# A four-layer graph network on one NeuronCore: about half of layer 3's dense products placed inside layer 2, with seven running-maximum blocks and 13 dense node tiles

## The chip, the cores and the metric

The kernel runs on one NeuronCore of a Trainium2 chip. Its engines are TensorE (PE: matrix products; PEld: the loading of the stationary operand), VectorE (DVE), ScalarE (ACT), GpSimd (POOL) and SyncE (SP). SP and ACT issue plain DMAs, POOL issues the indirect ones (gathers by a list of row numbers); all of them are carried by the same 16 DMA engines. The metric is device time in microseconds for one execution.

## What is computed

6250 nodes, 100 000 edges sorted by destination, features of 256, hidden width 512. A node's degree falls with its number (the destinations are drawn as the square of a uniform number), so the first nodes collect most of the edges of a tile.

```python
h = relu(layernorm(x))
h = sage_mean(h)   # h @ W1_self + mean over in-edges of h[src] @ W1_neigh + b1
h = sage_pool(h)   # hp = relu(h @ W2_pool + b2_pool); max over in-edges of hp[src];
                   # h @ W2_self + max @ W2_neigh + b2
h = sage_gcn(h)    # ((sum over in-edges of h[src]) + h) / (deg + 1) @ W3_neigh + b3
h = sage_mean(h)   # with W4_self, W4_neigh, b4
out = x + h @ W_fc + b_fc
```

Nothing nonlinear stands behind the maximum of layer 2, so the kernel multiplies the weights of layers 2 to 4 and the last one together beforehand: layer 3 works on a table of 512 columns that is the output of layer 2 times those products, layer 4 on one of 256.

## The kernel before

**Tiles.** The nodes make 49 tiles of 128 rows (NT), the edges 782 tiles of 128 (T). A table row that is summed on PE is kept as three bf16 parts (`parts`, L266: two ACT casts, two DVE subtractions), so each product over it is three matmuls: `tab_h` for layer 1, `tab_r` for layer 3 (3 x 512 columns, 3072 bytes a row), `tab_s` for layer 4 (3 x 256 columns).

**Two ways of summing edges (layers 1, 3 and 4).** The first node tiles, with many edges each, are *dense*: `build` (L280) makes, for a node tile d, the count matrix between its nodes and each source tile and writes it to the DRAM table `tab_a[d]`, 49 blocks of 128 x 128 bf16; `dense` (L401) then multiplies each block with the rows of source tile s, three matmuls for each s, and adds up over the 49 source tiles in one PSUM bank. The other node tiles are summed by `sums` (L337): for each edge tile POOL gathers the 128 source rows into a ring, DVE makes a one-hot matrix of the destinations, PE multiplies (three matmuls), four edge tiles share one PSUM bank (a group), and DVE adds the group into the node tiles that it may belong to. `HUB = (8, 9, 18)` gives the number of dense node tiles in layers 1, 3 and 4. The gathers of layer 3 thus begin at the edge group of node tile 9 (454 edge tiles), those of layer 4 at that of node tile 18 (314 edge tiles). The dense work is spread between the gathers by `Hub.advance` (L326); `wait` says after how many gathers it begins (40 in layer 3, 24 in layer 4).

**Layer 2 (L835 to L1080)** takes a maximum. For all 782 edge tiles POOL gathers 128 rows of 2 KB of `tab_p` (L1051) into a buffer `X` of two tiles (8 such buffers), DVE carries the running maximum (L1056), SP writes each pair to the DRAM table `runb` (512 KB, L1069). The edge tiles are cut into five blocks, `BLOCKS = (288, 208, 144, 88, 54)`. When a block is through, `block_end` (L1018) runs for it, in small steps beside the gathers of the next block, one step for each edge tile: `carry` (L937) passes the maximum across the block's partitions, `totals` (L979) gathers the result rows `tot` of each node tile that ends in the block and loads `th` from `tab_t`, and `done2` (L992) transposes them, makes the own part (`usA`, `usB`, L1005 and L1007) and the neighbour part (`un`, L1010) in fp32, splits the result into three parts and writes `tab_r[d]` (L1016). What has not run when the next block ends is issued then in one piece. The last block closes seven node tiles (42 to 48) behind the last gather. In layer 2 the builds of dense tiles 8 to 17 are placed too (L1061), and at its start the weight products (`products2`, L905).

**Layer 3 (L1122 on)** starts when `tab_r` is written: it loads all 49 tiles of it into SBUF (`resident`, L1113: seven DMAs of 2.7 MB on SP's queue), streams the dense blocks (`stream`, L1085: seven source tiles a DMA, on ACT's queue), and runs `sums` with the dense work of nine node tiles beside it. `done3` (L1134) adds the node's own row (three matmuls with an identity: L419 inside `dense` for dense tiles, L1142 for the others), writes `tab_s` and, with x added, `xq`. **Layer 4** does the same on `tab_s` with 18 dense tiles and writes `out`.

**Order.** The instructions are written down in the order of the Python code, and the framework's scheduler then fixes an order for each engine and each issuing queue, with times of its own for each instruction; every engine takes its instructions in that fixed order and waits for what is not ready.

Of the kernel before, what the change touches and what calls it, by code (L numbers as in the profile page):

```python
# [9 lines left out]
F32 = mybir.dt.float32  # L10
# [14 lines left out]
G = 4  # L25
BLOCKS = (288, 208, 144, 88, 54)
Z_SIGMA = 5.0
WIN = 8
HUB = (8, 9, 18)
# [38 lines left out]
def fast_path(  # L68
# [155 lines left out]
    def product(wp, pst, psm, w, rhs, put):  # L224
        k_n = w.shape[1] // P
        for m in range(w.shape[0] // P):
            wl = wp.tile([P, k_n * P], F32, name="wl", bufs=2)
            nc.scalar.dma_start(wl, w[m * P : (m + 1) * P, :])
            wT = wp.tile([P, k_n, P], F32, name="wT", bufs=2)
            pt = bank(pst, "pt", "pt_w", (k_n, P))  # L230
            for k in range(k_n):
                nc.tensor.transpose(pt[:, k, :], wl[:, k * P : (k + 1) * P], ident)
            nc.scalar.copy(wT, pt)
            pm = bank(psm, "pm", "pm_w", (rhs.shape[2],))
            for k in range(k_n):
                nc.tensor.matmul(pm, wT[:, k, :], rhs[:, k, :],
                                 start=(k == 0), stop=(k == k_n - 1))
            nc.scalar.copy(put[:, m, :], pm)
            yield
# [76 lines left out]
    class Hub:  # L316


        def __init__(self, work):
            self.work = [w if isinstance(w, tuple) else (None, w) for w in work]  # L320
            self.hot_at = [i for i, w in enumerate(self.work) if w[0]]
            self.done = 0
            self.hot = 0
            self.passed = 0

# [75 lines left out]
    def dense(d, block, rows, F, psd, todo, done, extra=0, self_term=False):  # L401

        hold = {}

        def run(s):
            if s == 0:
                hold[0] = bank(psd, "pd", "pd", (F + extra,))
            a = block(s)
            z = rows(s)
            for part in (2, 0, 1):  # L410
                c = extra if part == 2 else 0
                nc.tensor.matmul(hold[0][:, : F + c], a, z[:, part * F : (part + 1) * F + c],  # L412
                                 start=(s == 0 and part == 2),
                                 stop=(s == NT - 1 and part == 1 and not self_term))
            if s == NT - 1:
                if self_term:
                    z = rows(d)
                    for part in range(3):
                        nc.tensor.matmul(hold[0], ident_b, z[:, part * F : (part + 1) * F],  # L419
                                         start=False, stop=(part == 2))  # L420
                todo.append(done(d, hold[0]))

        return [lambda s=s: run(s) for s in range(NT)]
# [293 lines left out]
    with ExitStack() as on:  # L717
# [10 lines left out]
        def done1(d, acc):  # L728
# [23 lines left out]
            for k in range(KI):  # L752
# [11 lines left out]
        denses = [dense(d, lambda s, A=As[d % 2]: A[:, s, :], h0_row, FI, psd, todo, done1,  # L764
                        extra=1) for d in range(H1)]
# [68 lines left out]

    with tc.tile_pool(name="fl2c", bufs=1) as ck, ExitStack() as late:  # L835
        pst = late.enter_context(tc.tile_pool(name="pst2", bufs=2, space=PSUM))
        psm = late.enter_context(tc.tile_pool(name="psm2", bufs=3, space=PSUM))
# [96 lines left out]
        wpool = late.enter_context(tc.tile_pool(name="fw2", bufs=1))  # L934
        wk = late.enter_context(tc.tile_pool(name="fl2", bufs=2))

# [42 lines left out]
        def totals(d):  # L979
            tots = []  # L980
            for b in range(b_of[d][0], b_of[d][1] + 1):
                t = wk.tile([P, FH], F32, name="tot", bufs=6)
                nc.gpsimd.indirect_dma_start(
                    out=t, out_offset=None, in_=runs[b],
                    in_offset=bass.IndirectOffsetOnAxis(ap=rows_of[b][:, d : d + 1], axis=0),
                )
                tots.append(t)
            th = wk.tile([P, 2 * KI, P], F32, name="th2", bufs=3)
            nc.scalar.dma_start(th, tab_t[d].rearrange("p (k n) -> p k n", n=P))
            return tots, th  # L990

        def done2(d, got):  # L992
            tots, th = got
            hm = tots[0]
            for t in tots[1:]:
                nc.vector.tensor_tensor(hm, hm, t, op=ALU.max)
            pt = bank(pst, "pt", "pt_hTf", (KH, P))
            for j in range(KH):
                nc.tensor.transpose(pt[:, j, :], hm[:, j * P : (j + 1) * P], ident)
            hT = wk.tile([P, KH, P], F32, name="hTf")  # L1000
            nc.scalar.copy(hT, pt)  # L1001
            yield
            pm = bank(psm, "pm", "pm_prf")
            for k in range(KI):
                nc.tensor.matmul(pm, th[:, k, :], usA[:, k, :], start=(k == 0), stop=False)  # L1005
            for k in range(KI):
                nc.tensor.matmul(pm, th[:, KI + k, :], usB[:, k, :], start=False, stop=False)  # L1007
            yield
            for c in range(KH):
                nc.tensor.matmul(pm, hT[:, c, :], un[:, c, :], start=False, stop=(c == KH - 1))  # L1010
            pr = wk.tile([P, FH], F32, name="prf")
            nc.vector.tensor_add(pr, pm, prow)
            yield
            r3 = wk.tile([P, 3 * FH], BF16, name="r3")
            parts(pr, FH, r3)
            nc.sync.dma_start(tab_r[d * P : (d + 1) * P, :], r3)  # L1016

# [17 lines left out]
        steps = products2(wpool)  # L1035
        A = wk.tile([P, NT, P], BF16, name="A", bufs=1)
        work = []
        for d in range(H1, H4):
            work += build(d, A, (skR, mkR, RB1), wk, psb)
        hub = Hub(work)  # L1040
# [3 lines left out]
        for b, tb in enumerate(BLOCKS):  # L1044
            t0 = offs[b] // P
            for s0 in range(0, tb, G2):
                n = min(G2, tb - s0)
                X = wk.tile([P, G2, FH], F32, name="X2", bufs=8)
                for k in range(n):
# [13 lines left out]
                    hub.advance(math.ceil(len(work) * max(0, t - 60) / (T - 100)))  # L1063
# [15 lines left out]
        for _ in end:  # L1079
            pass  # L1080


    CH = 7

    def stream(pool, h, check):  # L1085

        got = {}

        def load(i):
            if i >= h * (NT // CH):  # L1090
                return
            d, c = divmod(i, NT // CH)
            t = pool.tile([P, CH, P], BF16, name="ac", bufs=5)
            nc.scalar.dma_start(t, tab_a[d, :, c * CH : (c + 1) * CH, :])
            got[d, c] = t
# [9 lines left out]
        def block(d, s):  # L1105
            c, r = divmod(s, CH)
            if r == 0:
                load(d * (NT // CH) + c + 4)
            return got[d, c][:, r, :]
# [3 lines left out]
    def resident(pool, table, F):  # L1113
        zt = pool.tile([P, NT, 3 * F], BF16, name="zt", bufs=1)
        for i0 in range(0, NT, CH):
            nc.sync.dma_start(  # L1116
                zt[:, i0 : i0 + CH, :],
                table[i0 * P : (i0 + CH) * P, :].rearrange("(c p) f -> p c f", p=P),
            )
        return zt  # L1120

    with ExitStack() as on:  # L1122
        ek = on.enter_context(tc.tile_pool(name="fe3", bufs=1))
        jb = g_of[H3][0] * G
        srcT = ek.tile([P, T - jb], I32, name="srcT3")
        nc.scalar.dma_start(srcT, stash_e[0, :, jb:T].bitcast(I32))
        keyT = ek.tile([P, T - jb], F32, name="keyT3")
        nc.scalar.dma_start(keyT, stash_e[1, :, jb:T])
        psd = on.enter_context(tc.tile_pool(name="psd3", bufs=2, space=PSUM))
        psg = on.enter_context(tc.tile_pool(name="psg3", bufs=3, space=PSUM))  # L1130
        psm = on.enter_context(tc.tile_pool(name="psm3", bufs=2, space=PSUM))

        with tc.tile_pool(name="fl3", bufs=2) as wk:
            def done3(d, acc):  # L1134
                q = wk.tile([P, FH], F32, name="q", bufs=2)
                if d < H3:
                    nc.vector.scalar_tensor_tensor(q, acc, rgcn[:, d : d + 1], qrow,
                                                   op0=ALU.mult, op1=ALU.add)
                else:
                    own = bank(psm, "pm", "pm_own")  # L1140
                    for part in range(3):
                        nc.tensor.matmul(own, ident_b, Z3[:, d, part * FH : (part + 1) * FH],  # L1142
                                         start=(part == 0), stop=(part == 2))
# [12 lines left out]
                nc.sync.dma_start(xq[d * P : d * P + n, :], xr[:n, :])  # L1156

            Z3 = resident(wk, tab_r, FH)
            block = stream(wk, H3, False)
            todo = []  # L1160
            work = []
            for d in range(H3):
                work += dense(d, lambda s, d=d: block(d, s), lambda s: Z3[:, s, :], FH, psd,
                              todo, done3, self_term=True)
            sums(wk, psg, tab_r, FH, srcT, keyT, jb, H3, done3, 7, Hub(work), wait=40, todo=todo)

        with tc.tile_pool(name="fl4", bufs=2) as wk:
# [9 lines left out]
            Z4 = resident(wk, tab_s, FO)  # L1177
            block = stream(wk, H4, True)
            todo = []
            work = []  # L1180
            for d in range(H4):
                work += dense(d, lambda s, d=d: block(d, s), lambda s: Z4[:, s, :], FO, psd,
                              todo, done4)
            sums(wk, psg, tab_s, FO, srcT, keyT, jb, H4, done4, 14, Hub(work), wait=24, todo=todo)
# [643 lines left out]
```

## Time and profile before

Three runs took 3241.90, 3242.98 and 3246.33 us (median 3242.98). The profiled execution took 3257.08 us, of which the span from the first to the last instruction is 3255.3 us.

| engine | busy us | share of the span |
|---|---|---|
| PE | 2334.0 | 72% |
| PEld | 1334.9 | 41% |
| DVE | 1858.8 | 57% |
| ACT | 887.4 | 27% |
| POOL | 2155.6 | 66% |

The stages, by the first and last gather of each: layer 1's gathers start at 145.2 and end at 788.7 us, layer 2's run from 827.5 to 2017.4, layer 3's from 2127.0 to 2795.0, layer 4's from 2815.0 to 3218.1.

In the profile an instruction is named by line, engine, operation and the tiles it writes and reads (out<-in). A PE matmul's duration is modelled and overlaps with its neighbours; the spacing of two of them is shorter. "PEclk" is the share of TensorE's clock that was granted. The DMA share is the mean busy share of the 16 DMA engines, and can exceed 1 a little, since packets overlap.

### The profile page before, as it was taken

How to read it: one execution, taken by the hardware profiler on the slowest of the kernel's cores; microseconds unless marked ns; L12 is line 12 of the kernel's file. 1: busy time of each engine (PE TensorE's matmuls, PEld its weight loads, DVE VectorE, ACT ScalarE, POOL GpSimd, SP SyncE). 2: the span in 40 equal slices, each digit the busy share in tenths (PEclk: the TensorE clock that was granted, in tenths of full speed). 3: DMA queues.
4: the chain of work that ended last, by engine and by line, in shares of the span. 5: the costliest groups of instructions: out<-in, count | busy, mean ns of one | idle time of the engine just before them, and what ended most of it. 6: DMA issues, size and time to landing. Idle time of an engine off the chain costs nothing. (4 is left out here: it accounts for less than half of the span.)

```text
span 3255.3 us, 39649 instructions
## 1 busy us (share of the span) xinstructions
PE 2334.0 (72%) x11991; PEld 1334.9 (41%) x12048; DVE 1858.8 (57%) x4764; ACT 887.4 (27%) x2367; POOL 2155.6 (66%) x2368
## 2 busy tenths in 40 slices
PE   2368999999483115410673677967999999799997
PEld 1134666666331002100231333422444444388886
DVE  4855666554656656655656665223566666566443
ACT  1557767663233223431234221200000000000000
POOL 5374777764567777777776776145766766577773
PEclk9678999999796556655786788989999999899999
DMA  5454677775999999999999999399999999888885
GB/s 178 162 156 139 212 217 222 241 221 177 324 386 405 394 386 375 409 399 382 380 397 407 393 406 388 119 355 355 346 336 340 345 338 352 289 288 271 259 263 167
DMA packets 394117, 991.17 MB, mean 304 GB/s; under 512 B 54799, under 2 KB 133729, under 8 KB 391558
## 3 DMA queue, kind: packets, MB, share of 16 engines
q0 software_dynamic: 155200, 557.74, 49.6%
q1 hardware_dynamic: 180788, 350.69, 28.6%
q10 hardware_dynamic: 57906, 80.12, 7.4%
q8 instruction: 98, 1.61, 0.2%
q14 instruction: 125, 1.02, 0.1%
HBM read 674.14 MB, written 315.00 MB: 304 GB/s over the span
## 5 line engine op out<-in xcount | busy, mean ns | idle before, releaser
L1051 POOL DMA_INDIRECT X<-tab_p,srcIf x782 | 836.0, 1069 | 314.5 <-issue 149.7
L374 PE MATMUL pg<-ring,hot 128*128 128x256 bf16 (+2 forms) x3697 | 780.5, 318 | 115.6 <-DMA ring<-tab_h,srcT 36.2
L412 PE MATMUL pd<-zt,ac 128*128 128x256 bf16 (+1 forms) x3944 | 696.5, 309 | 3.6 <-DMA zt<-tab_s 1.2
L302 PE MATMUL pb<-hm,hs 128*128 128x392 bf16 x781 | 280.4, 402 | 492.6 <-ACT A L306 292.7
L356 POOL DMA_INDIRECT ring<-tab_r,srcT x454 | 440.1, 969 | 277.4 <-PE pg L374 184.0
L356 POOL DMA_INDIRECT ring<-tab_h,srcT x474 | 452.1, 954 | 197.1 <-PE pg L374 80.5
L374 PEld LDWEIGHTS <-hot 128*128 128x128 bf16 x3726 | 367.7, 99 | 404.3 <-issue 175.7
L352 DVE TENSOR_SCALAR hot<-iota_bf,keyT 128x128 bf16<-128x128 bf16 x1242 | 310.2, 268 | 326.2 <-PE pg L374 314.1
L412 PEld LDWEIGHTS <-ac 128*128 128x128 bf16 x3969 | 389.4, 98 | 189.8 <-issue 3.4
L393 DVE SCALAR_TENSOR_TENSOR acc<-pg,M,acc 128x257 f32<-128x257 f32 (+2 forms) x567 | 306.9, 577 | 254.2 <-PE pg L374 253.5
L1056 DVE SCALAR_TENSOR_TENSOR X<-X,samef,X 128x512 f32<-128x512 f32 x386 | 289.4, 750 | 214.3 <-DMA X<-tab_p,srcIf 99.2
L1056 DVE SCALAR_TENSOR_TENSOR X<-X,samef 128x512 f32<-128x512 f32 x391 | 293.2, 750 | 184.8 <-DMA X<-tab_p,srcIf 181.0
L356 POOL DMA_INDIRECT ring<-tab_s,srcT x314 | 298.2, 950 | 125.0 <-PE pg L374 61.1
L294 ACT ACTIVATE hs<-ht,onef 128x128 bf16<-128x128 bf16 x781 | 289.8, 397 | 135.1 <-PE pb L302 134.4
L302 PEld LDWEIGHTS <-hs 128*128 128x128 bf16 x781 | 78.6, 105 | 597.7 <-issue 338.1
L306 ACT CAST A<-pb 128x392 bf16<-128x392 f32 x288 | 136.9, 480 | 438.1 <-DMA tab_a<-A 239.6
L1010 PE MATMUL pm_prf<-unf,hTf 128*128 128x512 f32 x392 | 198.6, 655 | 27.2 <-ACT hTf L1001 27.2
L296 DVE TENSOR_SCALAR hm<-iota_w,mk 128x392 bf16<-128x392 f16 x461 | 154.7, 341 | 62.5 <-PE pb L302 60.0
L269 ACT CAST q<-q 128x256 bf16<-128x256 f32 x49 | 19.8, 405 | 622.6 <-DVE q L1146 504.0
L412 PE MATMUL pd<-Z,A 128*128 128x256 bf16 (+1 forms) x1176 | 188.1, 274 | 0.1
L292 ACT ACTIVATE ht<-iota_bf,sk 128x128 bf16<-128x128 bf16 x461 | 171.8, 396 | 17.1 <-DVE bad L679 10.5
L1010 PEld LDWEIGHTS pm_prf<-unf,hTf 128*128 128x128 f32 x392 | 82.2, 214 | 148.2 <-issue 100.9
(272 smaller groups left out, 2321.0 us busy)
## 6 DMA issues: line engine op xcount, KB each, us to landing
runb<-X SPq DMA_DIRECT2D x391, 512.0 KB
ac<-tab_a ACTq DMA_DIRECT2D x189, 224.0 KB
tab_a<-A SPq DMA_DIRECT2D x18, 1568.0 KB
tab_r<-r SPq DMA_DIRECT2D x49, 384.0 KB
zt<-tab_r SPq DMA_DIRECT2D x7, 2688.0 KB
tab_t<-th SPq DMA_DIRECT2D x49, 256.0 KB
tab_p<-hpf SPq DMA_DIRECT2D x49, 256.0 KB
th<-tab_t ACTq DMA_DIRECT2D x49, 256.0 KB
```

The costliest lines, as they stand in the source:

```text
L292: nc.scalar.activation(t, iota_b, AF.Abs, bias=sk[:, r : r + 1])
L294: nc.scalar.activation(hots[0], t, AF.Relu, bias=one, scale=-1.0)
L296: nc.vector.tensor_scalar(hots[1], iota_w, mk[:, r : r + 1], None, op0=ALU.is_equal)
L302: nc.tensor.matmul(hold[0], hots[0], hots[1], start=(k == 0), stop=(k == k_of[w] - 1))
L352: nc.vector.tensor_scalar(hot[j], iota_b, keyT[:, j - jb : j - jb + 1], None, op0=ALU.is_equal)
L356: nc.gpsimd.indirect_dma_start(out=ring[:, j % deep, : 3 * F], out_offset=None, in_=table, in_offset=bass.IndirectOffsetOnAxis(ap=srcT[:, ...
L374: nc.tensor.matmul(pg[:, : F + c], hot[j], X[:, part * F : (part + 1) * F + c], start=(k == 0 and part == 2), stop=(k == n - 1 and part == 1),
L393: nc.vector.scalar_tensor_tensor(acc[d], pg, m, acc[d], op0=ALU.mult, op1=ALU.add)
L412: nc.tensor.matmul(hold[0][:, : F + c], a, z[:, part * F : (part + 1) * F + c], start=(s == 0 and part == 2), stop=(s == NT - 1 and part = ...
L1010: nc.tensor.matmul(pm, hT[:, c, :], un[:, c, :], start=False, stop=(c == KH - 1))
L1051: nc.gpsimd.indirect_dma_start(out=X[:, k, :], out_offset=None, in_=tab_p, in_offset=bass.IndirectOffsetOnAxis(ap=srcI[:, t : t + 1], axis=0),
L1056: nc.vector.scalar_tensor_tensor(X[:, k, :], prev, same[:, t : t + 1], X[:, k, :], op0=ALU.mult, op1=ALU.max,)
```

## The change

The first 24 of the 49 source tiles (EARLY) of layer 3's dense products are multiplied inside layer 2: as soon as four node tiles' rows `r3` are made (still in SBUF), `early_products` appends, for each of the 13 dense node tiles, one load of four blocks of `tab_a` (128 KB, on SP's queue) and four times three matmuls into a PSUM bank, and `add3` adds the bank to an SBUF accumulator `acc3[d]` (DVE; the first addition to each is an ACT copy). The own row of a dense tile goes into `acc3` the same way, so L419 goes. Layer 3 has 13 dense tiles (HUB 8, 13, 18), so its gathers begin at node tile 13: 386 edge tiles. It keeps 25 source tiles resident (five DMAs of 2.0 MB) and loads the own rows of node tiles 13 to 23 one by one (`zown`). There are seven blocks; the last closes node tiles 46 to 48, the one before it 41 to 45. The own parts of `done2` of the last eight node tiles are made in the middle of layer 2 (`own_terms`). Dense builds for tiles 8 to 12 are moved to the first 208 edge tiles. Three of the seven pieces of `tab_s` are loaded for layer 4 during layer 3, and layer 4's dense work begins with them, after 4 gathers instead of 24. Buffers change: X 8 to 6 pairs, `tot` 6 to 4, `th2` 3 to 2, PSUM banks `pm` 3 to 2 with two new ones for the early products, `wT` 2 to 1, `r3` 2 to 9.

```diff
-BLOCKS = (288, 208, 144, 88, 54)
+BLOCKS = (232, 184, 136, 100, 72, 38, 20)
-HUB = (8, 9, 18)
+HUB = (8, 13, 18)
+EARLY = 24
+OWN = 8
+OWN_AT = 64
...
+    def add3(d, v):
+
+        if d in begun:
+            nc.vector.tensor_add(acc3[d], acc3[d], v)
+        else:
+            begun.add(d)
+            nc.scalar.copy(acc3[d], v)
...
+        def own_terms():
+            for d in own:
+                th = load_th(d)
+                for _ in range(4):
+                    yield
+                pm = bank(psm, "pm", "pm_own2")
+                self_product(pm, th, True)
+                nc.vector.tensor_add(own[d], pm, prow)
+                yield
...
-            r3 = wk.tile([P, 3 * FH], BF16, name="r3")
+            if d < H3:
+                add3(d, pr)
+            r3 = early_pool[0].tile([P, 3 * FH], BF16, name="r3", bufs=2 * BATCH + 1)
             parts(pr, FH, r3)
             nc.sync.dma_start(tab_r[d * P : (d + 1) * P, :], r3)
+            if d < EARLY:
+                ready.append((d, r3))
+                if len(ready) == BATCH or d == EARLY - 1:
+                    early_products()
...
+                def load(d=d, got=got):
+                    got[0] = early_pool[0].tile([P, BATCH, P], BF16, name="ae", bufs=LOOK + 3)
+                    nc.sync.dma_start(got[0][:, : len(ss), :],
+                                      tab_a[d, :, ss[0] : ss[-1] + 1, :])
+
+                work = dense(ss, lambda s, got=got: got[0][:, s - ss[0], :],
+                             lambda s: batch[s], FH, psd, lambda v, d=d: add3(d, v))
+                early.add([(load, work[0])] + work[1:])
...
-                X = wk.tile([P, G2, FH], F32, name="X2", bufs=8)
+                X = wk.tile([P, G2, FH], F32, name="X2", bufs=6)
...
-                    hub.advance(math.ceil(len(work) * max(0, t - 60) / (T - 100)))
+                    if t > OWN_AT and t % 2:
+                        next(owns, None)
+                    if t <= begin:
+                        hub.advance(math.ceil(len(first) * max(0, t - 16) / (begin - 16)))
+                    else:
+                        hub.advance(len(first)
+                                    + math.ceil(len(rest) * (t - begin) / (T - 60 - begin)))
+                    early.advance(early.done
+                                  + max(1, math.ceil(early.left() / max(8, T - 30 - t))))
...
                 if d < H3:
-                    nc.vector.scalar_tensor_tensor(q, acc, rgcn[:, d : d + 1], qrow,
+                    nc.vector.tensor_add(q, acc, acc3[d])
+                    nc.vector.scalar_tensor_tensor(q, q, rgcn[:, d : d + 1], qrow,
                                                    op0=ALU.mult, op1=ALU.add)
                 else:
+                    if d in Z3:
+                        z = Z3[d]
+                    else:
+                        z = wk.tile([P, 3 * FH], BF16, name="zown", bufs=2)
+                        nc.sync.dma_start(z, tab_r[d * P : (d + 1) * P, :])
+                        yield 1
+                        yield 1
+                        yield 1
...
+                for s0, s1 in z4_early:
+                    if d == s1 - 1:
+                        Z4.update(resident(zk, tab_s, FO, s0, s1))
+            late_s = range(EARLY, NT)
...
-            sums(wk, psg, tab_r, FH, srcT, keyT, jb, H3, done3, 7, Hub(work), wait=40, todo=todo)
+            sums(wk, psg, tab_r, FH, srcE, keyE, jb, H3, done3, 7, Hub(work), wait=14, todo=todo)
...
-            sums(wk, psg, tab_s, FO, srcT, keyT, jb, H4, done4, 14, Hub(work), wait=24, todo=todo)
+            sums(wk, psg, tab_s, FO, srcE, keyE, jb, H4, done4, 14, Hub(work), wait=4, todo=todo)
```

## The prediction, made before the changed kernel was run

> **What bounds the kernel now.** I read the page's slices first, then the busy times by stage (stretches cut at the first and last gather of each stage; columns: stretch, length, then busy us and instruction count of each engine, granted PE clock, DMA share, GB/s), then the costs of single instructions, last the chain of waits where stages meet.
>
> ```profile
> PE   2368999999483115410673677967999999799997
> POOL 5374777764567777777776776145766766577773
> GB/s 178 162 156 139 212 217 222 241 221 177 324 386 405 394 386 375 409 399 382 380 397 407 393 406 388 119 355 355 346 336 340 345 338 352 289 288 271 259 263 167
> ```
> ```profile
> 1240.00:1975.00 735.00, 369.97 (x894) 155.10 (x893) 462.58 (x821) 221.58 (x602) 555.92 (x520) 0.70 1.03 394
> 2020.00:2127.00 107.00, 96.95 (x262) 45.00 (x261) 36.61 (x63) 23.93 (x42) 13.46 (x14) 0.97 0.44 155
> 2140.00:2250.00 110.00, 79.76 (x309) 30.54 (x314) 30.83 (x81) 0.81 (x2) 59.28 (x62) 0.94 1.02 400
> 2260.00:2795.00 535.00, 527.90 (x2404) 239.53 (x2452) 337.07 (x810) 35.30 (x88) 370.47 (x382) 1.00 0.96 341
> 2858.00:3236.00 378.00, 376.09 (x3444) 336.94 (x3444) 190.92 (x592) 0.00 (x0) 265.51 (x280) 1.00 0.83 258
> ```
>
> Layer 2 (first two lines above: 827 to 2127 us). While it gathers, PE is half idle, but two others are full: the DMA engines (share 1.03, 394 GB/s), and POOL, whose 520 indirect DMAs took 556 us and are 0.30 us apart at the least, so 712 of 735 us. Its gathers average 1.07 us against 0.95 in layer 4: in the trace's records those that overlap no two-input DVE instruction of L1056 take 0.96, those overlapped for over half 1.12 to 1.17. After the last gather (2017.4) 110 us pass until the first of layer 3 (2127.0), and that time is PE's:
>
> ```profile
> 2087.72 3.43 PE pm_prf L1010 x8
> 2091.15 0.44 PE pt_hTf L999 x4
> 2091.59 1.72 PE pm_prf L1005 x4
> 2093.31 1.72 PE pm_prf L1007 x4
> ```
> One node tile costs 0.44 + 3.44 (own part) + 3.43 (neighbour part) = 7.3 us, and some twelve stand in a row there.
>
> Layer 3 begins at the DMA limit (400 GB/s, while 19.3 MB of `zt` load) with one long wait, then from 2260 on PE is full at clock 1.00. Layer 4 loses its first 43 us to loads of `zt`, then PE is full again:
>
> ```profile
> 2223.42 30.24 DMA xq<-xrf
> ...
> 2796.85 0.65 PE pd L412 x3
> ...
> 2842.09 29.40 DMA zt<-tab_s
> ```
> The middle line gives the spacing of a 512-column matmul: 0.65 / 3 = 0.2157 us. In layer 4, (2646 + 942) matmuls of 256 columns at 0.1093 us (9 + 3 of them in 1.31 us on the chain) make 392 us.
>
> **Layer 3, part by part.** Gathers fall from 454 to 386, dense matmuls from 9 x 49 x 3 = 1323 (+27 own) to 13 x 25 x 3 = 975, own matmuls of the others from 120 to 108. PE: 975 + 3 x 386 + 108 = 2241 against 2832, at 0.2157 us 483 against 611. Two other bounds come close. POOL: 386 x (0.97 + 0.30) = 490 us (440.1/454 is this gather's mean). DMA: 386 gathers of 393 KB (151.8 MB), dense blocks 13 x 25 x 32.8 KB (10.7), `zt` 9.8, eleven `zown` 4.3, `tab_s`, `xrf`, `xq` 22.4, early `tab_s` pieces 4.1: 203 MB, against 235 now.
>
> Here a rule speaks against the change. The Trainium skill, "DMA: Bandwidth & Descriptors", Specifications, lets the HBM side bind at about 358 GB/s: 203 MB would take 567 us, and layer 3 could not go below some 585 with its ramps. The row above has 400 GB/s for 110 us, and layer 2 holds 394: by the row 508 us. The measurement decides; the rule's value stays in the range (-103 instead of -138).
>
> The sum, on PE: 483; 8 for the first gathers' latency; 25 idle while half as much `zt` as now shares the DMA engines (now: 133 us for 76 gathers that later take 1.40 each, so 27 lost, and 30 of them are the `xq` line, whose ACT wait stops DVE and PE); 10 for `zown`, asked for only three gathers ahead, behind `zt` on SP's queue, with PE's whole queue behind the matmul that waits (bounds 0, and 11 x 5 = 55 if each waits half of a backlogged 10 us landing); 9 to the next stage (2805.9 to 2815.0 now); 15 because PE, POOL and DMA (483, 490, 508) now lie so close that none hides another's waits. 550 us against 688 now (2127.0 to 2815.0): **-138** (bounds -155 and -95).
>
> **What layer 2 pays.** The early products are 13 x 24 x 3 = 936 matmuls; PE has 735 - 370 = 365 us free from 1240 to 1975. "TensorE: Matmul & The Clock Gate", Part 1, says that an idle PE runs at half clock, 426.7 ns for 512 columns: 400 us, which would not fit, and 35 us would be pushed behind the last gather. At the stretch's granted 0.70 they take 936 x 0.2157 / 0.70 = 288 and fit; in slices where PE is busy three quarters of the time the clock was 0.86. I take the row: nothing on the path.
> Their loads are 78 of 128 KB, 10.2 MB; seven blocks add 4 `tot` gathers and 4 carry DMAs, 2.1 MB. At 394 GB/s that is 31 us, beside which POOL's 8 more issues (11 us) fit. Bounds: 0, as the fastest slice moved 409; 31. I take 31, as 1.03 leaves no room.
> DVE gets 78 additions and 8 for the own terms at 0.69 us (the L1012 addition): 59 us, 63% to 71% busy; PE's own-term products move without growing. Both are hidden, if they come in time.
> Six X buffers instead of eight: a buffer lives from its gather to the landing of its write, by the trace's records 9.2 us to the write's issue and some 7 to land, together 17.1 (median; upper quartile 19.7). Eight pairs at 1.41 us a tile allow 22.6 us, six 16.9. POOL already waited for `runb` 36 times (19.1 us). If lives shrink as fewer are in flight, the cost is 0; if they keep at 18.3 on average, 18.3/12 - 1.41 = 0.115 us a tile, 90 us. The additions also stand in DVE's queue ahead of L1056, and the block loads in SP's queue ahead of `runb` writes: where PE is late, the X chain waits. I take 25 for all this, nearer 0, since much of 17.1 us is queueing that fewer buffers shorten. Layer 2's gathers: **+56** (+15 to +120).
>
> **The tail of layer 2.** In order behind the last gather PE now has twelve node tiles (88 us) and the landings around them. After: of block five (33 to 40) five to six tiles are left when block six ends 20 gathers (28 us) earlier, so 40 us of PE work starts about 20 us before the last gather; then 41 to 45 and 46 to 48 at 7.3 - 3.44 = 3.9 us each, 31 us. The end at -20 + 40 + 31 = 51, then `r3` and its landing (2120.4 to 2127.0 now: 7) and 4 of waits: 62 against 110: **-48** (-60 to -30). What is late next is the last block's carry (scan, `fix` gather, scatter, `tot`: some 25 us), just covered by 41 to 45.
>
> **Layer 4.** 392 of PE plus 6 for the first gather plus 10 for the four remaining pieces (5.5 MB, 14 us at 400, behind gathers): 408 against 421 (2815 to 3236): **-13** (-25 to 0). The early pieces wait on SP for `tab_s` writes (3.65 us on the chain), with `xq` writes behind them.
>
> Single buffers of `wT`, two `th2`, two `pm` banks and more setup for blocks touch work that ends before anyone needs it: 0.
>
> **Sum.** +56 - 48 - 138 - 13 = -143. From the profiled 3257.1 that is 3114, from the median 3243 it is **3100**.
>
> **Rivals.**
> (a) *Layer 2's in-order waits win; slower.* Place: the six X buffers. For it: buffers live 17.1 us against 16.9 allowed, POOL has no slack to catch up, and three queues get waits on PE ahead of the X chain. Against: DVE and SP have idle time, and the scheduler places the work where its operands should be ready. From the gains of 199 us, (life/12 - 1.41) x 782 must exceed 199: from a mean life of 20.0 us on it is slower, close to today's upper quartile. At 20.5 it costs 234: 3278.
> (b) *Layer 3 is held by transfers.* It keeps its 341 GB/s of today: 203/341 = 595, with 9 to the next stage 604, so -84 instead of -138: 3154. Against: 341 was what PE asked for.
> (c) *The early products don't fit.* PE at half clock, 35 us pushed into the tail, and sums late on DVE for as much again: 3170.
> (d) *No gain left:* pieces of (a) to (c) that just cancel, 3243.
>
> **Chances.** Forecast 0.60 (its own range 3050 to 3150), (b) 0.13, (c) 0.09, (a) 0.14, (d) 0.04. Slower and faster count from 0.2% (6.5 us), about what runs that spread by 4 us can tell from no change. Faster 0.82, same 0.04, slower 0.14. The range goes up over (b) and (c), and some way to a layer 2 that loses 140: 3040 to 3225.
>
> **What would show it.** Right: gathers of layer 2 end 40 to 80 us later than 2017 with POOL still over 95% taken; under 75 us to layer 3's first gather, PE chains of 3.9 us a tile; layer 3's gathers 1.30 to 1.35 us apart, PE still over 0.9 busy; no 30 us `zt` wait at layer 4's start. Wrong: POOL idle before L1051 released by `runb` or DVE over 100 us; DVE additions into `acc3` waiting for PE by several us each; early matmuls behind the last gather; layer 3 above 600 us with PE idle.

## The result: no difference, and the profile after

The changed kernel took 3246.4 us (median of 12 runs), the kernel before 3244.0 beside it: a ratio of 1.0001, 95% interval 0.9988 to 1.0014. The forecast was 3100. The profiled execution took 3249.5 us, its span 3247.5. The profile of the kernel before caught an execution 13 us above its median (3257.1 us), so the sum below falls by 8 where the medians agree; where those 13 us lie can't be seen, and a stage's change can be off by as much. Stages are cut at their first and last gather, as in the prediction:

| stage, us | before | after | change | predicted |
|---|---|---|---|---|
| start to first X gather | 827.5 | 851.5 | +24 | 0 |
| X gathers of layer 2 | 1189.9 | 1250.0 | +60 | +56 |
| last X gather to layer 3's first (the tail) | 109.6 | 166.2 | **+57** | **-48** |
| layer 3, to layer 4's first gather | 688.0 | 553.2 | -135 | -138 |
| layer 4, to the end of the span | 440.3 | 426.6 | -14 | -13 |
| sum | 3255.3 | 3247.5 | -8 | -143 |

Layer 3 gave what was promised. It was spent in layer 2: 60 us in the gathers, which was forecast, 57 in the tail, which was to shrink, and 24 before the first gather. Of the 135 us that are missing against the forecast, 105 are the tail's and 24 the setup's.

Stretches of the changed kernel (columns: stretch, length, busy us and instructions of PE, PEld, DVE, ACT and POOL, granted PE clock, DMA share, GB/s):

```profile
core 0: us, PE busy (x) PEld busy (x) DVE busy (x) ACT busy (x) POOL busy (x), PEclk, DMA share, GB/s
...
1700.00:2101.00 401.00, 287.78 (x894) 128.32 (x893) 241.37 (x399) 75.63 (x176) 273.92 (x263) 0.84 1.00 370
2101.00:2267.00 166.00, 137.50 (x412) 65.17 (x411) 62.69 (x114) 33.73 (x58) 25.86 (x27) 0.91 0.38 129
2267.00:2821.00 554.00, 503.06 (x2241) 219.96 (x2241) 341.94 (x852) 39.66 (x98) 376.22 (x387) 0.96 0.98 368
```

The last stretch of the gathers in the kernel before:

```profile
1700.00:2017.00 317.00, 195.30 (x483) 85.99 (x482) 201.65 (x355) 93.44 (x236) 233.91 (x221) 0.77 1.03 399
```

Read the first two rows of the changed kernel together. Over the last 401 us of the gathers PE is busy for 288, so it has 113 us to spare; then the tail begins, the gathers have stopped, the DMA share falls to 0.38, and PE has 137 us of work in 166. PE idles first and is the bound afterwards. The chain of waits shows with what (start, us, what):

```profile
2124.84 7.12 PE pd L426 x33
2131.97 0.44 PE pcf L989 x4
2132.40 9.71 PE pd L426 x45
2142.11 0.44 PE pt_hTf L1051 x4
2142.55 1.72 PE pm_prf L1026 x4
2144.27 1.72 PE pm_prf L1028 x4
2145.99 3.43 PE pm_prf L1060 x8
...
2202.60 2.74 DMA runb<-fixf,fixIf
2207.38 0.95 POOL tot L1012
2208.63 3.62 DMA tot<-runb,rows_of
2212.28 0.70 DVE tot L1048
```

After the last X gather (2101.5), PE first finishes node tiles 30 to 32, then runs 78 early matmuls (2124.84 to 2142.1), and only then begins with node tile 33, at 7.3 us a tile, of which eight stand in a row (33 to 40, block five). The last gather of block five was issued at 2000, but its carry was late too: its transposes (`pcf`, 2131.97) stand behind 33 of the early matmuls, and the scatter that writes the carried maximum back to `runb`, ahead of the `tot` gathers of all eight, runs on POOL only then:

```profile
2133.41 1.00 POOL L1000 DMA_INDIRECT runb<-fixf,fixIf  x1 [30.96 <-DVE fixf L999]
```

Then PE waits twice for the carry of a later block (the `fixf` scatter, then `tot`; the first time is shown), 10 us each.

Two more pairs of lines, at the start of layer 3 and of layer 4:

```profile
2269.08 16.54 DMA ac<-tab_a
...
2294.86 42.68 DMA zown<-tab_r
```
```profile
2822.25 12.10 DMA ac<-tab_a
2834.37 26.30 DMA zt<-tab_s
```

The `zown` loads queue behind `zt` on SP as feared, but once only (43 us, not eleven times); with it layer 3 still took 553 us against the predicted 550, at 368 GB/s in the stretch row above. At layer 4's start the wait for `zt` was to go; 26 us of it are still on the chain.

### The profile page after: what moved, and what is told of

It is laid out like the page before. It is cut to its first block, busy times and chain, and to the rows that moved or that the text cites. A ratio compares the mean times of both kernels' runs of the same rounds, so it can differ in the third digit from the quotient of the medians.

```text
span 3247.5 us, 40515 instructions
## 1 busy us (share of the span) xinstructions
PE 2435.1 (75%) x12413; PEld 1381.5 (43%) x12413; DVE 1877.6 (58%) x4846; ACT 894.9 (28%) x2380; POOL 2077.2 (64%) x2308
## 4 chain that ended last, share of the span: by engine, by line
DMA 34%; PE 25%; POOL 6%; issue 5%; DVE 4%; SPq 0%; ACT 0%; ACTq 0%; POOLq 0%; DVEq 0%
DMA X<-tab_p,srcIf 17%; PE pd L426 13%; PE pg L388 8%; DMA runb<-X 7%; POOL X L1133 4%; DMA ring<-tab_r,srcE 3%; PE pm_prf L1060 2%; DVE X L1138 2%; DMA zown<-tab_r 1%; DMA ac<-tab_a 1%; DMA zt<-tab_s 1%; POOL ring L370 1%; DMA tot<-runb,rows_of 1%; DMA runb<-fixf,fixIf 1%; PE pm_prf L1026 1%
## 5 line engine op out<-in xcount | busy, mean ns | idle before, releaser
L388 PE MATMUL pg<-ring,hot 128*128 128x256 bf16 (+2 forms) x3522 | 725.4, 315 | 76.7 <-DMA ring<-tab_h,srcT 35.1
L426 PE MATMUL pd<-zt,ac 128*128 128x256 bf16 (+1 forms) x3621 | 611.8, 303 | 27.0 <-DMA ac<-tab_a 15.2
L370 POOL DMA_INDIRECT ring<-tab_r,srcE x386 | 376.2, 975 | 183.1 <-PE pg L388 79.6
L388 PEld LDWEIGHTS <-hot 128*128 128x128 bf16 x3522 | 347.9, 99 | 331.5 <-issue 141.9
L426 PEld LDWEIGHTS <-ac 128*128 128x128 bf16 x3621 | 355.9, 98 | 171.8 <-issue 24.3
L407 DVE SCALAR_TENSOR_TENSOR acc<-pg,M,acc 128x257 f32<-128x257 f32 (+2 forms) x538 | 287.2, 567 | 224.2 <-PE pg L388 223.5
L370 POOL DMA_INDIRECT ring<-tab_s,srcE x314 | 297.9, 949 | 119.3 <-issue 55.8
L426 PE MATMUL pd<-r,ae 128*128 128x512 bf16 x936 | 242.2, 403 | 108.8 <-DVE acc L857 75.2
L366 DVE TENSOR_SCALAR hot<-iota_bf,keyE 128x128 bf16<-128x128 bf16 x700 | 170.1, 270 | 186.1 <-PE pg L388 178.3
L426 PEld LDWEIGHTS <-ae 128*128 128x128 bf16 x936 | 95.4, 102 | 246.5 <-issue 162.3
```

What stands on the lines that cost most here:

```text
L366: nc.vector.tensor_scalar(hot[j], iota_b, keyT[:, j - jb : j - jb + 1], None, op0=ALU.is_equal)
L370: nc.gpsimd.indirect_dma_start(out=ring[:, j % deep, : 3 * F], out_offset=None, in_=table, in_offset=bass.IndirectOffsetOnAxis(ap=srcT[:, ...
L388: nc.tensor.matmul(pg[:, : F + c], hot[j], X[:, part * F : (part + 1) * F + c], start=(k == 0 and part == 2), stop=(k == n - 1 and part == 1),
L407: nc.vector.scalar_tensor_tensor(acc[d], pg, m, acc[d], op0=ALU.mult, op1=ALU.add)
```

## The experiments

Four theories were set up. **1**: the early products' PE time made the fixed order put the node tiles late, and the chip keeps to that order. **2**: the small last blocks with their carries make the tail long. **3**: six X buffers make the gathers slow. **4**: setup for seven blocks delays the first X gather.

The first four kernels ran on a chip on which the kernel before takes 3674.9 us; their ratios are to that kernel on that chip, and their stages are compared only with each other. All later ones ran on two chips where it takes 3246.7 and 3245.1.

### Taking parts out of the order

**No early products.**

```diff
-            if d < EARLY:
-                ready.append((d, r3))
-                if len(ready) == BATCH or d == EARLY - 1:
-                    early_products()
```

> The changed kernel without its early products: the sums of node tiles 0 to 12 over source tiles 0 to 23 are left out (no block loads, no 936 matmuls, no 78 additions; acc3 gets only the own rows). Theory 1 (the early matmuls fill PE in the scheduler's planned time, so that node tiles are put late in the fixed order): 12 node tiles instead of 18 behind the last X gather, so from last X gather to first layer 3 gather 85 to 100 us instead of 166; X gathers 1205 to 1230 us instead of 1250; layer 3 unchanged at 553 +- 8; total 3125 to 3150. Theory 2 (the small last blocks and their carries make the stretch long): still over 150 us there, total 3195 to 3225. Theory 3 (six X buffers make the X gathers slow): X gathers stay above 1240.

Ratio to before 0.9717 (0.9662 to 0.9772); the tail took 90.2 us, the X gathers 1285. For theory 1, against 2: blocks, carries and buffers are all there, and the tail is short.

**Node tiles first.** Each step of the node tiles and carries is emitted inside

```diff
+                    with tc.high_priority(1000):
                         if todo and s0 + k > 8:
                             try:
                                 next(todo[0])
...
```

> The changed kernel with all its work, but the node tiles' and the carries' instructions in layer 2 are given to the scheduler with a higher priority (1000), so that they stand in the fixed order near where the code issues them. Theory 1: 12 node tiles behind the last X gather, that stretch 90 to 110 us instead of 166, X gathers within 15 us of 1250, layer 3 unchanged; total 3175 to 3195. Theory 2 (small blocks and carries): stretch over 150, total 3235 to 3250. A third possibility: the early matmuls and sums now come late and hold DVE and X, so that X gathers grow by 30 or more and the total stays above 3215.

Ratio 0.9887 (0.9828 to 0.9947), tail 129.6, X gathers 1308. Half right. Node tiles 0 to 37 now stand before the last X step on DVE, but it was the early matmuls that went late instead: 261 of them are recorded behind the last X step, the last one at 2527, 128 us behind the last X gather at 2399. Priority moved the lateness from the one to the other.

**The old blocks.**

```diff
-BLOCKS = (232, 184, 136, 100, 72, 38, 20)
+BLOCKS = (288, 208, 144, 88, 54)
```

> The changed kernel with the five blocks of before (288, 208, 144, 88, 54), all else kept. Theory 1: the order is still late and with larger last blocks later, 24 node tiles behind the last X gather: stretch 180 to 220 us; total 3240 to 3290. Theory 2: the stretch goes back to about 110, total 3170 to 3200. Theory 4 (setup for seven blocks delays the first X gather, 851 instead of 828): first X gather at 826 to 835, i.e. some 20 us less there; if it stays at 850, something else delays it.

Ratio 1.0036 (1.0014 to 1.0058), tail 221.1 us: theory 2 is reversed, the small blocks are what kept the tail from being longer. The first X gather came 57 us behind the last gather of layer 1, against 62 in the two runs before: only a quarter of what theory 4 needed.

**Eight buffers.**

```diff
-                X = wk.tile([P, G2, FH], F32, name="X2", bufs=6)
+                X = wk.tile([P, G2, FH], F32, name="X2", bufs=8)
-OWN = 8
+OWN = 4
```

> The changed kernel with eight X buffers as before instead of six, and for the room only four own terms made ahead instead of eight. Theory 3 (six buffers cost the X gathers 25 us or more, as the prediction put it): X gathers 1225 or less instead of 1250, stretch behind them longer by 14 us (4 x 3.44), total 3225 to 3240. If the +60 is bytes and DVE work alone: X gathers within 8 us of 1250, total 3250 to 3265.

Ratio 0.998 (0.9959 to 1.0001), X gathers 1292, tail 185. On this chip there was no run of the unaltered kernel to hold 1292 against, so this one decided nothing about the buffers, which were taken up again below. Its first X gather came 57 us behind layer 1, with seven blocks.

### The order alone

**The changed kernel once more**, as a ground for its parts.

> The changed kernel itself, unaltered, so that the parts have a ground on the chip they run on. On the chip of the first runs I expect it within 0.5% of the kernel before, X gathers 1285 to 1310 us, and 165 to 180 us from the last X gather to the first of layer 3 (scaled from its first profile and from the run with eight buffers); on a chip like the first one 3247, 1250 and 166.

3245.6 us, ratio 0.9995 (0.9983 to 1.0007); first X gather at 850.6, gathers 1257.3, tail 166.0, layer 3 548.3, layer 4 425.3.

**A third of the matmuls, all loads and additions.**

```diff
-            for part in (2, 0, 1):
+            for part in ps:
...
-                             lambda s: batch[s], FH, psd, lambda v, d=d: add3(d, v))
+                             lambda s: batch[s], FH, psd, lambda v, d=d: add3(d, v),
+                             ps=(2,))
```

> The changed kernel with one of the three matmuls of each early product (hi and mid parts are left out, 312 matmuls instead of 936); the 78 block loads, the 78 additions on DVE, the buffers, the blocks are all kept. Theory 1 (PE time of the early products makes the order late): 12 node tiles behind the last X gather as without any early product, that stretch within 10 us of the 90 measured there. If it is the additions or loads that hold the node tiles up: stretch over 150 as in the unaltered kernel. X gathers: if the early products' PE time slows them, back to those without early products (1285 on the first runs' chip); if loads and additions do, as in the unaltered kernel.

3179.7 us, tail 90.7, as with none at all. The 78 loads, 78 additions, all buffers and blocks are there, so what makes the node tiles late is the matmuls' PE time. X gathers 1246.3: 11 us less than with all, which is little beside the 7 us between the two profiles of the unaltered kernel (1250.0 and 1257.3).

**The order pinned.** All work is kept. A dependency without a semaphore puts the addition that ends a node tile ahead of a given X step on DVE:

```diff
+                        while made and made[0][0] + 8 <= t:
+                            tc.add_manual_dep(
+                                ins.ins, made.pop(0)[1].ins.name,
+                                mybir.DependencyInfo(mybir.DependencyClass.NoSync,
+                                                     mybir.DependencyReason.DATA),
+                                reason="order",
+                            )
```

(`ins` is the X step of tile t; `made` holds the additions of node tiles 0 to 32 with the t at which each was emitted.)

> The changed kernel with all its work and one thing added: for node tiles 0 to 32 the order of DVE is fixed so that the addition that ends a node tile stands at most 8 X steps behind where the code issues it. Theory 1 with PE having room on the chip: node tiles 30 to 32 and the 78 early matmuls no longer stand behind the last X gather, stretch 110 to 130 us, X gathers longer by less than 15 us; total 35 to 50 us under the unaltered kernel. Rival (PE has no room late in the gathers, since its work comes only when the blocks end): the X steps now wait for PE, X gathers grow by 30 to 60, what the stretch loses they gain, total within 15 us of the unaltered kernel.

3182.5 us, ratio to before 0.9806 (0.9776 to 0.9835), 63 us under the unaltered kernel; tail 94.6 instead of 166.0, X gathers 1257.1 instead of 1257.3. Nothing but the order differs, and the gathers paid nothing for it. From the trace's records, how many of the 775 X steps DVE had done when it made the addition of a node tile:

```
node tile                  8    12    16    22    26    29    32    behind the last step
unaltered                469   513   598   665   736   769   775    30 to 48
no early products        467   498   594   640   695   718   739    37 to 48
a third of the matmuls   466   495   595   645   690   715   737    37 to 48
pinned                   469   497   595   638   701   719   725    37 to 48
```

(The expectations speak of 18 tiles; by these records it is 19.) In the unaltered kernel neighbouring node tiles stand 10 to 13 X steps apart from tile 23 on, in the others mostly 6 to 8, near the 6 at which the code emits them; by tile 32 that makes 50 steps against the pinned kernel, 80 us at 1.6 us a step. The gathers did not grow when the lag was taken out, so it was a matter of the order and not of PE's speed. The carry of block five moved with the node tiles; its scatter ran 88 us earlier than in the unaltered kernel:

```profile
2045.02 1.35 POOL L1000 DMA_INDIRECT runb<-fixf,fixIf  x1 [0.30 <-DVE X L1142]
```

The same two stretches and the early matmuls (first and last start) show it from PE's side, pinned kernel:

```profile
1700.00:2110.00 410.00, 330.65 (x1055) 152.80 (x1070) 256.32 (x440) 80.36 (x179) 287.42 (x273) 0.90 1.01 379
2110.00:2204.00 94.00, 62.64 (x164) 29.89 (x164) 36.04 (x59) 21.71 (x37) 14.52 (x15) 0.81 0.37 136
```
```profile
L426 PE MATMUL pd<-r,ae x907: 376/379/634, 1281.8 to 2050.3; 128*128 128x512 bf16 x182
...
  DVE acc L857: 20.4, 13
```

and the early matmuls of the unaltered one:

```profile
L426 PE MATMUL pd<-r,ae x936: 376/379/634, 1281.5 to 2141.7; 128*128 128x512 bf16 x188
...
  DVE acc L857: 75.2, 24
```

In the last 410 us of the gathers PE now does 331 us of work, not 288 of 401, the last early matmul starts at 2050 and not at 2142, and PE's waits for DVE's additions fall from 75 to 20 us. A granted clock of 0.90 in place of 0.84 goes with the fuller PE.

**Pinned, builds early, room of its own for X.**

```diff
-                                    + math.ceil(len(rest) * (t - begin) / (T - 60 - begin)))
+                                    + math.ceil(len(rest) * (t - begin) / (420 - begin)))
...
+        xk = late.enter_context(tc.tile_pool(name="fx2", bufs=6))
         segments()
...
-                X = wk.tile([P, G2, FH], F32, name="X2", bufs=6)
+                X = xk.tile([P, G2, FH], F32, name="X2")
```

> As the pinned kernel, with two more changes: the one-hot blocks of node tiles 13 to 17 are built by gather 420 instead of by gather 722, which takes their PE time out of the late part; and the X tiles get room of their own, opened before the segments' setup, so that the first X gather need not wait until the setup's tiles are free. Theory 4 (the setup for seven blocks delays the first X gather): first X gather 15 to 25 us earlier against the stage before it than in the unaltered kernel; otherwise no difference. Theory 1 with PE short late: X gathers 10 to 30 us shorter than in the pinned kernel. Total 60 to 90 us under the unaltered kernel.

3179.6 us: no more than pinned. Both additions failed. Building earlier shortened nothing. The first X gather came 22 us earlier, and most of it was lost again at once; POOL in the changed kernel and then in this one:

```profile
788.79 0.95 POOL L370 DMA_INDIRECT ring<-tab_h,srcT  x1 [0.69 <-PE pg L388]
851.52 1.02 POOL L1133 DMA_INDIRECT X<-tab_p,srcIf  x1 [61.78 <-DVE nr L808]
```
```profile
786.46 0.95 POOL L370 DMA_INDIRECT ring<-tab_h,srcT  x1 [0.67 <-PE pg L388]
827.18 0.95 POOL L1137 DMA_INDIRECT X<-tab_p,srcIf  x1 [39.77 <-DMA srcIf<-sflat]
...
841.00 0.95 POOL L1137 DMA_INDIRECT X<-tab_p,srcIf  x1 [0.30 <-issue]
852.49 0.24 POOL L795 IOTA nr<- 128x128 f32 x1 [10.54 <-issue]
856.07 0.98 POOL L1137 DMA_INDIRECT X<-tab_p,srcIf  x1 [3.34 <-DVE nr L799]
```

With room of its own the first gather waits for its list of rows, 40 us instead of 62. So it was the place of the X tiles, on room that the setup still held, that made it late. But after twelve gathers (six buffers) POOL stands still from 842 to 856: DVE is still with the setup and frees no buffer. Counted from the last gather of layer 1, the gain on the pinned kernel was 9 us at gather 60 and nothing at the last one (1319.4 and 1319.7 us behind it).

### Where the gathers' 60 us come from

**Six buffers in the kernel before**, nothing else.

```diff
-                X = wk.tile([P, G2, FH], F32, name="X2", bufs=8)
+                X = wk.tile([P, G2, FH], F32, name="X2", bufs=6)
```

> The kernel before with six X buffers instead of eight and nothing else changed. Theory 3 (six buffers slow the X gathers, the prediction's 25 of its +56): X gathers 1215 instead of 1190, the rest as before, total 20 to 30 us over before; if the buffers are the whole of the +67 that the changed kernel shows, 1250. If lives shrink with fewer in flight: within 6 us of 1190.

3299.0 us, ratio 1.0165 (1.0142 to 1.0189); X gathers 1231.4 instead of 1189.9. The medians lie 54 us apart, the two profiled spans 43. What POOL waited for before an X gather (us, times), in the kernel before, then with six buffers, then in the changed kernel:

```profile
its engine sat idle before it (us, times) until:
...
  DVE X L1056: 30.4, 78
...
  DMA runb<-X: 19.1, 36
```
```profile
  DVE X L1056: 70.1, 90
  DMA runb<-X: 42.9, 93
```
```profile
  DVE X L1138: 88.4, 98
  DMA runb<-X: 63.0, 81
```

A buffer comes free when its write to `runb` has landed, or when DVE has gone through it; both waits doubled.

**Seven blocks in the kernel before**, nothing else (`BLOCKS` of the change).

> The kernel before with the seven blocks of the change and nothing else changed. Theory 4: the first X gather comes 20 to 25 us later after the last gather of layer 1 (62 instead of 39), for the setup of two more blocks. X gathers: 11 us more if the eight further POOL transfers and their 2 MB cost what they take, none if hidden. Behind the last X gather 12 node tiles of 7.3 us stand instead of 14: 100 to 115 us against 110, if the carries of the small blocks hold nobody up; over 125 if they do (theory 2).

3257.3 us, ratio 1.0040 (1.0026 to 1.0054). First X gather 38.5 us behind layer 1 (38.8 before): theory 4 falls. X gathers 1191.3 (1189.9), tail 99.8 (109.6). The median is 12 us longer, the profiled span, 3254.0, is not, since the profile of before was of an execution 13 us above its median; in which stage the 12 us lie stays open.

**No early products, again.**

> The changed kernel without its early products once more (sums of node tiles 0 to 12 over source tiles 0 to 23 left out), to have its X gathers on a chip where the unaltered kernel's are known: there 1257, and 1246 with a third of the matmuls. If the loads of 10.2 MB cost what they take at 394 GB/s: 1215 to 1228. If only the matmuls' PE time counts: 1238 to 1246. Stretch behind the last gather 90 as measured.

3148.2 us, ratio 0.9699 (0.9675 to 0.9724); X gathers 1230.6, tail 88.1. Between the two expectations: with all early products the gathers take 1257.3, so these cost 26.7, of which 11.0 go with two thirds of the matmuls, the rest with loads, additions and the last third.

41.5 for six buffers, 1.4 for the blocks and 26.7 for the early products make 69.6; measured were 1257.3 - 1189.9 = 67.4. This agreement is closer than the figures allow, since each is a difference of two single profiles. Nor is a part worth the same in every kernel, as the next run shows.

**Pinned, with eight buffers** (and four own terms for the room).

> The pinned kernel with eight X buffers, and for the room four own terms made ahead instead of eight. If six buffers cost the X gathers 25 us: 1232 instead of 1257, the stretch behind them 10 to 14 us longer (4 x 3.44), total 10 to 15 us under the pinned 3182. If they cost nothing: 1250 to 1262, total 10 to 14 us over it.

**3154.3 us, ratio to before 0.9717 (0.9691 to 0.9743): faster than both kernels.** X gathers 1228.0 instead of 1257.1, the tail 104.2 instead of 94.6. With the early products (and four own terms fewer) two buffers are thus worth 29 us, where they were worth 41.5 in the kernel before. POOL's waits for buffers:

```profile
  DVE X L1142: 50.4, 69
  DMA runb<-X: 27.0, 53
```

## Why the prediction was wrong

**The step that failed is the tail: -48 predicted, +57 measured**, and in it one sentence: "of block five (33 to 40) five to six tiles are left when block six ends". It took the place at which the code emits a node tile for the place at which the chip runs it. In the fixed order 19 node tiles' additions, 78 early matmuls and the carry of block five stood behind the last X step. The price per tile (7.3 and 3.9 us) was right; their number was not. (Its count for the kernel before was low as well: by the same records 14 additions, not twelve.) The pinned kernel, with that order put right, brings the tail from 166.0 to 94.6 and 63 us to the total. Two of the prediction's own signs of being wrong came: early matmuls behind the last gather, and POOL idle before X gathers for 151 us (88.4 + 63.0) where 100 was the mark.

**Early products, "nothing on the path".** Whether 936 matmuls fit was asked of PE's busy time on the chip, by the granted clock. They do fit there: the pinned kernel runs all of them during the gathers, which stay at 1257. The Trainium skill's rule of the idle clock ("TensorE: Matmul & The Clock Gate", Part 1), by which 35 us would have overflowed, did not bind: in the last stretch of the gathers the granted clock, 0.77 in the kernel before, rose with the work to 0.84 and, pinned, 0.90. What the step left out is that the scheduler fixes the order before the chip runs anything, with times of its own. That the matmuls did not fit by those times is inferred; shown is that PE time alone moves the order (a third of the matmuls: 12 tiles behind, not 19), that priority trades one lateness for another, and that pinning the order takes 71 us off the tail with all the work kept. Rival (c) had part of the picture, work pushed behind the last gather, but by half a clock. Rival (d) is nearest in number (3243), by luck: most of what cancels the gain is the order, which it does not name.

**What is left of the tail's error.** Even pinned it takes 94.6 us, not 62. PE's timeline, pinned kernel:

```profile
2137.19 0.60 PE L989 MATMUL pcf<-identf,cTf 128*128 128x128 f32 x4
2137.62 0.60 PE L970 MATMUL ptcf<-identf,X 128*128 128x128 f32 x4
2147.11 1.08 PE L1051 MATMUL pt_hTf<-identf,tot 128*128 128x128 f32 x4 [8.88 <-DVE tot L1048]
2149.57 0.48 PE L1051 MATMUL pt_hTf<-identf,tot 128*128 128x128 f32 x1 [1.38 <-DVE tot L1048]
...
2172.53 0.60 PE L989 MATMUL pcf<-identf,cTf 128*128 128x128 f32 x4
2182.87 1.51 PE L1051 MATMUL pt_hTf<-identf,tot 128*128 128x128 f32 x6 [9.74 <-DVE tot L1048]
```

Two carry chains leave PE idle for 8.9 + 1.4 and 9.7 us. The last block's carry was not "just covered by 41 to 45", since its transposes (`pcf`, 2172.53) stand in PE's order behind those tiles; block six's (2137.19) stand behind tile 40 in the same way. The change had also taken away what PE did meanwhile. In the kernel before, the own parts of the next tiles run while a carry is under way; made ahead, they leave PE nothing to do. PE's waits for `tot` in the tail (us, times, longest), first in the kernel before with seven blocks, then in the pinned kernel with four own terms made ahead (the one with eight buffers), then with eight:

```profile
PE pt_hTf L999 <- DVE tot L996: 5.7, 3, 2.9
```
```profile
PE pt_hTf L1051 <- DVE tot L1048: 14.5, 3, 9.7
```
```profile
PE pt_hTf L1051 <- DVE tot L1048: 20.0, 3, 9.7
```

So of the 27.5 us (8 x 3.44) that the own terms were to save, some 14 (20.0 - 5.7) came back as waiting. By the chain the 94.6 are 28 to the end of tile 40, 12 of waiting, 20, 14 of waiting, 14 and 7; predicted were 20, 31 for the two groups together, 7, and 4 of waits.

**Gathers, +56: right, in part by luck.** Buffers were put at 25 with all in-order waits and cost 41.5 in the kernel before, 29 in the pinned one; the 31 us of further bytes were an upper bound, and all that the early products add, the matmuls' part included, is 27. The mechanism of rival (a) was at work, at a fifth or less of the 199 us that it needed to decide.

**Setup, "0": missed by 24 us.** Seven blocks don't cost it; the changed layout does, which set X on room still in use. Its worth is less than 24, since DVE's setup holds the gathers anyway.

**Layer 3, -138: right (-135 and, in the second profile, -140).** "DMA: Bandwidth & Descriptors", Specifications, of the Trainium skill has about 358 GB/s as the HBM limit of a NeuronCore, half of a stack's 716; it would have made this stage -103. The one core at work here held 368 over the whole stretch. The measurement stands, and rival (b) falls. The 35 us set aside for `zt` and `zown` came as one wait of 43.

**Layer 4, -13: right in sum only.** The `zt` wait that was to go is still 26 us long. From the first gather to the last matmul the stage gained 7 us (423.3 to 416.1); the other 6.5 lie behind the last matmul, where nothing was predicted.

**Slips of the working that change nothing.** 0.65 / 3 is 0.2167 and not 0.2157, which makes the 483 us 486; and 30 us of an `xq` line can't be a part of 27 lost.

## What to carry to other kernels

When work is moved into the idle time of an engine, ask twice whether it fits: on the chip, and in the order that is fixed beforehand. Here an order planned around a full engine lagged, and the lag stayed although the chip had the time: look for an engine that idles in one stage and is the bound of the next, and count, in the trace of the engine that runs both, how many steps of the one chain stand ahead of each step of the other. Pinning 33 instructions cost the gathers nothing here (1257.1 against 1257.3 us). Ask of work that is taken out of a chain whether it was covering a wait. Buffers given up for the new work are to be priced by an experiment of their own, in the kernel that will have it: two of eight cost here as much as the moved work itself (29 to 41 us against 27).

## What the runs showed of the hardware unasked

Chips differ by more than the changes here, and not evenly. The kernel without early products took 3148 us on one chip and 3578 on another. Up to the last gather of layer 1 it took 1029 us in place of 788, over half of the difference; its X gathers were 4% longer (1231 and 1285 us), its layer 4 16%; stretches of layer 4, on the slower and on the other chip:

```profile
3074.00:3567.00 493.00, 423.43 (x3588) 349.83 (x3588) 207.94 (x660) 0.00 (x0) 297.31 (x314) 0.97 0.74 222
```
```profile
2718.00:3144.00 426.00, 398.77 (x3590) 353.73 (x3590) 212.26 (x664) 0.00 (x0) 297.71 (x314) 0.96 0.82 257
```

POOL and DVE are busy for the same time, PE for 6% more, and the rest is time in which PE runs nothing, at the same granted clock. The profile names no cause for it. The runs on each chip were made in one batch, so the chip and the time of the run can't be told apart. A part of a change is to be compared on the chip it ran on.
